# Masked attention with an int8 linear layer: maxima from float32 q and k in row groups, jobs in column groups, fixed PSUM banks

## The chip, the core and the metric

The kernel runs on one core of a Trainium2 chip. Five engines work side by side, each through its own queue in order: TensorE (PE in the profile; its weight loads are PEld), VectorE (DVE), ScalarE (ACT), GpSimd (POOL) and SyncE (SP), which issues most DMAs. PSUM, where TensorE writes its results, has eight banks of 128 partitions x 512 float32. The metric is the device time of one execution in microseconds (us), less being better; it is given as the median of several runs.

## The reference

Eight batches of x (512 channels x 1024 tokens) go through attention with 16 heads of 32 channels under a key mask; the result is quantised per row to int8, multiplied by an int8 weight, scaled, and added to x.

```python
Q, K, V = (proj(Wq), proj(Wk), proj(Wv))           # (B, 16, 1024, 32) each
att = einsum('bhqd,bhkd->bhqk', Q, K) / sqrt(32) + b
att = att * m + (1.0 - m) * -1e30
y = einsum('bhqk,bhkd->bhqd', softmax(att), V)     # back to (B, 512, 1024)
q, in_scale = per_token_quant_int8(y)              # absmax / 127 of each row
out = einsum('bsk,nk->bsn', q, weight) * in_scale * w_scale + bias
return x + out.astype(float16)
```

## The kernel before

**Tiling.** Four heads (128 channels) of one batch are a group: 8 x 4 = 32 groups. A group has two halves X of 512 queries, and a half has eight steps, one for each chunk of 128 keys: 512 steps s in all, 16 to a group. The main loop (L907) goes by pairs of steps.

**A step.** `scores` (L433) writes four heads' scores, keys on partitions, into two tiles of two banks. For each head a bfloat16 matmul with ones (L450) first puts in the query's maximum (`shift`, split into three bfloat16 parts), then a float32 matmul adds k times q (L455). The heads lie in four groups of 32 rows of the array, so four matmuls run abreast. ACT takes the exponential of 128x1024 at a time (L464) into e. `add_up` (L476) adds the e of a half on POOL, 128x2048 at a time, in seven of its eight steps. `product` (L489) multiplies by V, each head in its own group of 32 columns, accumulating over the eight steps of a half in one bank. `half_denominators` (L505) sums the columns of the half's sum; DVE copies (L515), takes reciprocals (L543) and multiplies y (L546).

**Maxima ahead of the scores.** The query's maximum over the keys must be known before its scores are. `maxima` (L371) computes the scores once more with queries on partitions, in units of one head and 128 queries: two matmuls over all 128 rows in float32r. For that q and k are split into a high and a low part (`evict`, L236: ACT writes the high part and the full one, DVE the low part), and DMAs stack them into 128 rows per head (`stack_head`, L339, ks and qs). `take_maxima` (L402) is one DVE operation per unit, which adds the mask and reduces 1024 keys, with the result read out of an accumulator by a second, small instruction. A step has two units. `split_tops` (L422, L424) cuts a half's maxima into three bfloat16 parts on POOL, and `place_tops` transposes them by a DMA on SP (L429).

**Jobs.** The projections of later groups (`project`, L211, `project_v`, L311) and the linear layer of the group before last (`linear`, L716) are cut into pieces and laid between the maxima, as matmuls over the full array. One piece of a pair runs in column groups instead (`columns`, L199), behind the product. Float32 matmuls appear as two instructions each. ACT or DVE move the results out of PSUM. Later steps quantise y on ACT (L595 to L601), and POOL adds bias and x (L699, L700).

**Order.** All five engines run in the order in which the program is written (`manual_schedule`). PSUM is four pools: two tiles of two banks for scores and some maxima (ps_s), one of two banks for other maxima and the denominators (ps_m), one bank for the product (ps_av), one for jobs (ps_job).

Of the kernel before, what the change touches and what calls it, by code (L numbers as in the profile page):

```python
# [20 lines left out]
P = 128  # L21
# [3 lines left out]
QUARTER = 256  # L25
# [8 lines left out]
def kernel(  # L34
# [15 lines left out]

# [11 lines left out]
    UH = HG * HN  # L83
    last = n_groups - 1
    ON_ARRAY = n_steps - NT - HN
    BY_TURNS = n_steps - NT - 2
# [3 lines left out]
    xpool = ctx.enter_context(tc.tile_pool(name="x", bufs=5))  # L90
    mpool = ctx.enter_context(tc.tile_pool(name="mask", bufs=2))
    qkpool = ctx.enter_context(tc.tile_pool(name="qk", bufs=2))
    stack = ctx.enter_context(tc.tile_pool(name="stack", bufs=4))
    epool = ctx.enter_context(tc.tile_pool(name="e", bufs=3))
    small = ctx.enter_context(tc.tile_pool(name="small", bufs=2))
    work = ctx.enter_context(tc.tile_pool(name="work", bufs=1))
    ps_s = ctx.enter_context(tc.tile_pool(name="ps_s", bufs=2, space=PSUM))
    ps_m = ctx.enter_context(tc.tile_pool(name="ps_m", bufs=1, space=PSUM))
    ps_av = ctx.enter_context(tc.tile_pool(name="ps_av", bufs=1, space=PSUM))
    ps_job = ctx.enter_context(tc.tile_pool(name="ps_job", bufs=1, space=PSUM))  # L100

    def bank(name, dtype=F32, shape=(P, HALF)):
        return ps_job.tile(list(shape), dtype, tag="job", name=name)


# [8 lines left out]
    def load_w(i, which):  # L114
        cols = slice(i % NG * P, (i % NG + 1) * P)
        name, src = (("wq", wqT), ("wk", wkT))[which]
        w = const.tile([P, NG, P], F32, tag=name, name=f"{name}_{i}")
        nc.sync.dma_start(w, src[:, cols].rearrange("(c p) o -> p c o", p=P))
        w_qk[i, which] = w
# [32 lines left out]
    bias_sb = const.tile([P, N], F32, tag="bias", name="bias_sb")  # L152

# [8 lines left out]

# [8 lines left out]

# [17 lines left out]


    full = {}
    splits = {}

    def columns(acc, weights, moving, **kwargs):

        for r in range(0, P, DH):
            nc.tensor.matmul(acc[r : r + DH], weights[:, r : r + DH], moving, **kwargs)  # L199

    def project(i, which, h, quarters=(0, 1), by_chunk=False):


        b, g = divmod(i, NG)
        w = w_qk[i, which]

        def piece(a, c, matmul=nc.tensor.matmul):
            acc = jobs["bank"]
            cols = slice(a * QUARTER, (a + 1) * QUARTER)
            place = slice((a - quarters[0]) * QUARTER, (a - quarters[0] + 1) * QUARTER)  # L210
            matmul(  # L211
                acc[:, place],
                w[:, c, :],
                x_sb[b, c][:, h * HALF : (h + 1) * HALF][:, cols],
                start=(c == 0 and (a == 0 or not by_chunk)),
                stop=(c == NG - 1 and (a == quarters[-1] or not by_chunk)),
            )
            if (a, c) == (quarters[-1], NG - 1):
                cols = slice(quarters[0] * QUARTER, (a + 1) * QUARTER)
                evict(i, which, h, cols, acc[:, : place.stop])  # L220

        order = [(a, c) for a in quarters for c in range(NG)]
        if by_chunk:
            order.sort(key=lambda o: o[1])
        return [lambda *x, a=a, c=c: piece(a, c, *x) for a, c in order]

    def split_tiles(i, which, h):
        name = "qk"[which]
        high = work.tile([P, HALF], F32R, tag=f"{name}h{h}", name=f"{name}h_{i}_{h}")
        low = work.tile([P, HALF], F32R, tag=f"{name}l{h}", name=f"{name}l_{i}_{h}")  # L230
        splits[i, which, h] = high, low
        full[i, which, h] = qkpool.tile(
            [P, HALF], F32, tag=f"{name}{h}", name=f"{name}f_{i}_{h}"
        )

    def evict(i, which, h, cols, acc):  # L236
        if (i, which, h) not in splits:
            split_tiles(i, which, h)
        high, low = (t[:, cols] for t in splits[i, which, h])
        top = masks[i // NG][1]  # L240
        for dst in (high, full[i, which, h][:, cols]):
            if which == 0:
                nc.scalar.activation(dst, acc, AF.Copy, scale=top)  # L243
            else:
                nc.scalar.copy(dst, acc)

        early = jobs["early"]

        def rest():
            if early:  # L250

                f = full[i, which, h][:, cols]
                nc.gpsimd.tensor_tensor(low, f, high.bitcast(F32), ALU.subtract)
            elif which == 0:
                nc.vector.scalar_tensor_tensor(
                    low, acc, top, high.bitcast(F32), ALU.mult, ALU.subtract
                )
            else:
                nc.vector.tensor_tensor(low, acc, high.bitcast(F32), ALU.subtract)

        later.append(rest)

    def first_projections():

        k0, k1 = (ps_s.tile([P, HALF], F32, tag="s", name=f"kps_0_{h}") for h in range(NH))
        accs = [(0, 0, bank("qps_0")), (1, 0, k0), (1, 1, k1)]

        order = [(c, a) for c in (0, 1) for a in accs[1:]] + [(c, accs[0]) for c in (0, 1)]
        order += [(2, a) for a in accs[1:] + accs[:1]] + [(NG - 1, a) for a in accs]

        warm = ps_av.tile([P, P], F32, tag="av", name="warm")
        for _ in range(WARM):
            nc.tensor.matmul(warm, ones_b, ones_b, start=True, stop=True)
# [8 lines left out]
        top = masks[0][1]  # L282
        for which, h, acc in accs:
            split_tiles(0, which, h)
            f = full[0, which, h]
            if which == 0:
                nc.scalar.activation(f, acc, AF.Copy, scale=top)
            else:
                nc.vector.tensor_copy(f, acc)
        prepare_mask(0, 2)  # L290
        for which, h, _ in accs[1:] + accs[:1]:
            high, low = splits[0, which, h]
            nc.scalar.copy(high, full[0, which, h])
            nc.gpsimd.tensor_tensor(low, full[0, which, h], high.bitcast(F32), ALU.subtract)
# [3 lines left out]
    def project_v(i, quarters, offset=0):  # L298

        b, g = divmod(i, NG)  # L300
        KQ = QUARTER // P

        def piece(a, r, matmul=nc.tensor.matmul):
            if i not in v_sb:
                v_sb[i] = work.tile([P, NT, P], F32, tag="v", name=f"v_{i}", bufs=2)
            acc = jobs["bank"]
            t, part = divmod(r, 2)
            k = a * KQ + t
            place = offset + (k - quarters[0] * KQ) * P
            for c in range(part * NG // 2, (part + 1) * NG // 2):  # L310
                matmul(  # L311
# [6 lines left out]
            if (a, r) == (quarters[-1], 2 * KQ - 1):  # L318
                keys = slice(quarters[0] * KQ, (a + 1) * KQ)
                copies.append(  # L320
                    lambda: nc.scalar.copy(  # L321
                        v_sb[i][:, keys, :].rearrange("p k c -> p (k c)"),
                        acc[:, offset : place + P],
                    )
                )

                if offset == 0:
                    flush(copies)

        return [lambda *x, a=a, r=r: piece(a, r, *x) for a in quarters for r in range(2 * KQ)]  # L330

    stacks = {}

    def stack_tile(i, j, which):
        stacks[i, j, which] = stack.tile(
            [P, T], F32R, tag="qk"[which], name=f"{'qk'[which]}s_{i}_{j}"
        )

    def stack_head(i, j, which, h, engine=nc.sync):  # L339
        order = ((0, 0, 1, 1), (0, 1, 0, 1))[which]  # L340
        if (i, j, which) not in stacks:
            stack_tile(i, j, which)
        s = stacks[i, j, which]
        for a, part in enumerate(order):
            engine.dma_start(  # L345
                s[a * DH : (a + 1) * DH, h * HALF : (h + 1) * HALF].bitcast(F32),
                splits[i, which, h][part][j * DH : (j + 1) * DH, :].bitcast(F32),
            )

# [3 lines left out]
    def maxima_bank(k):  # L353


        first = k < -FIRST * HN
        turn = k < HALF_FIRST and k % 3 != 1
        pool, tag = (ps_s, "s") if (turn if first else k % HN in (1, 2)) else (ps_m, "m")
        return pool.tile([P, NH, HALF], F32, tag=tag, name=f"mps_{k}")

    def maxima(k):
        X, u = divmod(k, UH)
        i, h = divmod(X, NH)
        j, n = divmod(u, HN)
        q, kk = stacks[i, j, 0], stacks[i, j, 1]
        if u == 0:
            tops[X] = small.tile([P, HN, HG], F32, tag="tops", name=f"tops_{X}")
        acc = maxima_bank(k)
        n0 = h * HN + n
        for a in range(NH):  # L370
            nc.tensor.matmul(  # L371
                acc[:, a, :],
                q[:, n0 * P : (n0 + 1) * P],
                kk[:, a * HALF : (a + 1) * HALF],
                start=True,
                stop=True,
            )
        take_maxima(k, acc, X, j, n)
# [667 lines left out]
```

## Time and profile before

| what | value |
|---|---|
| median of 3 runs | 2527.62 us (2527.54 to 2527.64) |
| profiled execution, first to last instruction | 2525.2 us |
| TensorE, clock granted over the span | 0.999 of full speed |
| scores of the first step start | 46.05 us |
| last exponential starts | 2503.3 us |
| first sum of a half (POOL), 63 records | from 53.5 to 2450.7 us |
| one exponential (ACT, 128x1024) | 1111 ns, 1024 of them |
| one sum (POOL, 128x2048) | 4566 ns |
| one maximum (DVE, 128x1024) | 1224 ns, 1024 of them |
| one reciprocal (DVE, 128x128) | 924 ns, 252 of them |

"Busy" is the time in which an engine has an instruction under way; the matmuls' ends are modelled, so a run of matmuls is best measured from one start to the next. A group of instructions is shown as line, engine, operation, what is written and read with shapes, count, busy time in us and mean ns of one, and behind the last bar the idle time of the engine before them, with what ended it.

### The profile page before, as it was taken

To read this page: it belongs to the slowest core of one execution; us is meant where nothing else is said; L and a number is where in the kernel's file an instruction comes from. 1 tells how busy PE (TensorE), PEld (TensorE's weight loads), DVE (VectorE), ACT (ScalarE), POOL (GpSimd) and SP (SyncE) were. 2 spreads that over 40 slices of the span, in tenths; PEclk is the share of its full clock that TensorE was granted. 3 is DMA by queue.
4 is the path that set the end of the run, shared out by engine and by line. 5 is a ranking of instruction groups with operands and counts; after the bars stand their busy time and mean duration, and the time that the engine had idled before them with its cause. 6 is when DMAs were issued, how large, how long until landed. Compare 5 with 4: busy or idle time off the path is not lost.

```text
span 2525.2 us, 50860 instructions
## 1 busy us (share of the span) xinstructions
PE 2500.8 (99%) x19444; PEld 1431.3 (57%) x19444; DVE 1805.5 (71%) x2901; ACT 1474.3 (58%) x1653; POOL 2245.5 (89%) x906
## 2 busy tenths in 40 slices
PE   9999999999999999999999999999999999999998
PEld 5555555555556565555555555655555555555542
DVE  5567777777777777777777777777776777777775
ACT  3556666556665556665556665566655566556654
POOL 2988999999999999999999999999999999999992
PEclk9999999999999999999999999999999999999999
DMA  5333333343333433334333343333433334333331
GB/s 160 81 80 96 96 88 83 88 113 85 90 77 92 113 79 86 89 91 113 80 83 92 85 117 82 77 87 96 116 81 79 83 102 107 86 78 81 83 76 45
DMA packets 225953, 228.10 MB, mean 90 GB/s; under 512 B 104368, under 2 KB 138160, under 8 KB 225712
## 3 DMA queue, kind: packets, MB, share of 16 engines
q1 hardware_dynamic: 225136, 224.06, 34.6%
q8 instruction: 156, 2.56, 0.4%
q10 hardware_dynamic: 576, 0.79, 0.1%
q14 instruction: 85, 0.70, 0.1%
HBM read 57.70 MB, written 16.78 MB: 29 GB/s over the span
## 4 chain that ended last, share of the span: by engine, by line
POOL 67%; PE 20%; issue 11%; SPq 1%; DMA 1%; ACT 1%; DVE 0%; POOLq 0%; DVEq 0%
POOL sum L476 58%; PE mps L371 4%; PE av L489 4%; PE sps L455 3%; PE job L211 3%; POOL o L700 3%; POOL o L699 3%; PE job L311 2%; PE sps L450 2%; POOL part L422 1%; POOL tops L424 1%; PE job L716 1%; SPq L345 1%; PE job L199 0%; PE dps L505 0%
## 5 line engine op out<-in xcount | busy, mean ns | idle before, releaser
L476 POOL TENSOR_TENSOR sum<-sum,e 128x2048 f32<-128x2048 f32 x374 | 1707.9, 4566 | 28.6 <-ACT e L464 9.5
L402 DVE CUSTOM_DVE_ANT_0 rest<-mps,row 128x1024 bf16<-128x1024 f32 x1024 | 1253.3, 1224 | 597.8 <-PE mps L371 363.0
L464 ACT ACTIVATE e<-sps,kbias 128x1024 f32<-128x1024 f32 x1024 | 1085.7, 1111 | 451.4 <-PE sps L455 425.0
L371 PE MATMUL mps<-ks,qs 128*128 128x512 f32 x2032 | 763.7, 457 | 8.6 <-ACT e L464 7.0
L455 PE MATMUL sps<-qf,kf 32*128 32x512 f32 x4096 | 549.5, 589 | 0.0
L489 PE MATMUL av<-e,v 128*32 128x512 f32 x4096 | 494.3, 598 | 0.0
L371 PEld LDWEIGHTS mps<-ks,qs 128*128 128x128 f32 x2032 | 332.7, 190 | 235.5 <-DVE den L515 94.5
L476 POOL TENSOR_TENSOR sum<-e,e 128x2048 f32<-128x2048 f32 x63 | 286.4, 4546 | 140.7 <-ACT e L464 137.9
L489 PEld LDWEIGHTS av<-e,v 128*32 128x32 f32 x4096 | 107.4, 109 | 346.0 <-issue 345.0
L311 PEld LDWEIGHTS job<-wv,x 128*128 128x128 f32 x1884 | 258.1, 191 | 27.3
L311 PE MATMUL job<-wv,x 128*128 128x128 f32 x1884 | 260.1, 274 | 0.0
L211 PE MATMUL job<-x,wq 128*128 128x256 f32 x914 | 246.4, 378 | 0.0
L450 PE MATMUL sps<-shift,ones_b 32*128 32x512 bf16 x2048 | 229.0, 383 | 3.2 <-DVE tops L402 1.4
L543 DVE RECIPROCAL den<-den 128x128 f32<-128x128 f32 x252 | 224.9, 924 | 0.0
L211 PE MATMUL job<-x,wk 128*128 128x256 f32 x854 | 223.8, 378 | 0.0
L455 PEld LDWEIGHTS sps<-qf,kf 32*128 32x128 f32 x4096 | 207.4, 183 | 4.5
L211 PEld LDWEIGHTS job<-x,wq 128*128 128x128 f32 x914 | 172.3, 189 | 34.3
L321 ACT COPY v<-job 128x256 f32<-128x256 f32 (+1 forms) x95 | 41.8, 442 | 253.4 <-PE job L311 253.4
L211 PEld LDWEIGHTS job<-x,wk 128*128 128x128 f32 x854 | 161.2, 189 | 30.8
L450 PEld LDWEIGHTS <-ones_b 32*128 32x128 bf16 x2048 | 69.4, 91 | 182.1 <-issue 164.4
L243 ACT ACTIVATE qh<-job,top 128x256 fp32r<-128x256 f32 (+1 forms) x91 | 49.8, 547 | 174.5 <-PE job L211 149.1
L716 PE MATMUL job<-w_sb,qT 128*128 128x256 bf16 (+1 forms) x944 | 126.4, 276 | 0.0
(110 smaller groups left out, 1439.8 us busy)
## 6 DMA issues: line engine op xcount, KB each, us to landing
ks<-kh SPq DMA_DIRECT2D x508, 64.0 KB, 2.0
ks<-kl SPq DMA_DIRECT2D x508, 64.0 KB, 2.0
qs<-qh SPq DMA_DIRECT2D x506, 64.0 KB, 2.0
qs<-ql SPq DMA_DIRECT2D x506, 64.0 KB, 2.0
x<-in_x SPq DMA_DIRECT2D x32, 512.0 KB, 4.9
xr<-in_x SPq DMA_DIRECT2D x62, 256.0 KB, 3.4
out<-o SPq DMA_DIRECT2D x62, 256.0 KB, 3.3
wk<-in_wkT SPq DMA_DIRECT2D x32, 256.0 KB, 3.7
```

The lines of the kernel that those rows point to most:

```text
L211: matmul(acc[:, place], w[:, c, :], x_sb[b, c][:, h * HALF : (h + 1) * HALF][:, cols], start=(c == 0 and (a == 0 or not by_chunk)), stop=( ...
L311: matmul(acc[:, place : place + P], x_sb[b, c][:, k * P : (k + 1) * P], wv_sb[:, c, g * P : (g + 1) * P], start=(c == 0), stop=(c == NG - 1),)
L371: nc.tensor.matmul(acc[:, a, :], q[:, n0 * P : (n0 + 1) * P], kk[:, a * HALF : (a + 1) * HALF], start=True, stop=True,)
L402: nc.vector.tensor_tensor_reduce(out=rest, in0=acc.rearrange("p h t -> p (h t)"), in1=row, scale=-1.0, scalar=HIGH, op0=ALU.add, op1=ALU.m ...
L450: nc.tensor.matmul(accs[j // 2][:, j % 2, :], ones_b[r, :], shift[r, :], start=True, stop=False)
L455: nc.tensor.matmul(accs[j // 2][:, j % 2, :], k[r, k0 * P : (k0 + 1) * P], q[r, :], start=False, stop=True,)
L464: nc.scalar.activation(e[:, 2 * a : 2 * a + 2, :], acc, AF.Exp, bias=kbias[:, kc : kc + 1], scale=SCALE)
L476: nc.gpsimd.tensor_tensor(sums[X], other, exps[s], ALU.add)
L489: nc.tensor.matmul(accs_av[X][r, :], v_sb[i][:, kc, r], exps[s][:, j, :], start=(kc == 0), stop=(kc == NT - 1),)
L543: nc.vector.reciprocal(d[:, cols], source[:, cols])
L699: engine.tensor_tensor(o16[:, c], o[:, c], bias_sb[:, half][:, c], ALU.add)
L716: matmul(acc, qT[:, k, :], w8_sb[:, k, half][:, cols], start=(k == 0), stop=(k == NT - 1),)
```

## The change

**PSUM.** One pool holds four tiles of a single bank (one[0] to one[3]) and two tiles of a pair of banks (two[0], two[1]) for the whole run. An even step's scores go to one[0], one[1] and two[1], an odd step's to one[2], one[3] and two[1]; the maxima of that step go to the other two singles and to two[0]. When the exponentials have read a step's singles, the product of an even step takes the first, and the step's job the other one.

**Maxima.** Each step has one unit of two heads and 128 queries: four float32 matmuls of 32 rows straight from q and k, behind the scores. For the second half of the keys they read copies in which the heads are turned by 64 rows (`turn_heads`, three copies per group, two DMAs each), so that the four matmuls use four row groups. The splits, the stacks and their DMAs are gone. Maxima run LEAD = 11 steps ahead of the scores. Where a head's two halves lie in single banks, DVE takes them in two operations, one into tops[X][0] and one into tops[X][1]; the latter is first filled by a memset on POOL. `split_tops` moves from POOL to DVE and starts with the smaller of the two.

**Jobs and product.** The product of two steps is made in every even step, into a fresh bank; ACT copies the first of a half into y, and DVE adds the other three. All jobs run in column groups, behind the product in even steps (linear, denominators) and behind the maxima in odd ones (three pieces of 128 columns of projections). ACT copies the denominators. The exponential is three operations: two of one bank, one of a pair. e has five buffers in place of three, x eight in place of five, weights two in place of one. From eleven steps before the end on, no maxima are left, and products and denominators are made step by step.

```diff
-    ps_s = ctx.enter_context(tc.tile_pool(name="ps_s", bufs=2, space=PSUM))
...
+    psum = ctx.enter_context(tc.tile_pool(name="psum", bufs=1, space=PSUM))
+    one = [psum.tile([P, HALF], F32, tag=f"one{a}", name=f"one{a}") for a in range(4)]
+    two = [psum.tile([P, NH, HALF], F32, tag=f"two{a}", name=f"two{a}") for a in range(2)]
+    def score_banks(s):
+        a = 0 if s >= TAIL else s % 2
+        return one[2 * a : 2 * a + 2], two[1 - s % 2 if s >= TAIL else 1]
+    def maxima_banks(s):
...
+        return [one[2:] if s % 2 == 0 else one[:2], halves(two[0])]
...
+        for a in range(2):
+            nc.sync.dma_start(t[a * 2 * DH : (a + 1) * 2 * DH, :], f[(1 - a) * 2 * DH : (2 - a) * 2 * DH, :])
...
+    def project(i, which, h, cols, acc):
+        b, g = divmod(i, NG)
+        for c in range(NG):
+            columns(
+                acc,
+                w_qk[i, which][:, c, :],
+                x_sb[b, c][:, h * HALF : (h + 1) * HALF][:, cols],
+                start=(c == 0),
+                stop=(c == NG - 1),
+            )
...
+    def maxima(m, accs):
+        X, u = divmod(m, NT)
+        i, h = divmod(X, NH)
+        pair, n = divmod(u, HN)
+        for a in range(NH):
+            turn = a if m >= EARLY else 0
+            q = turned[i, 0][h] if turn else full[i, 0, h]
+            k = turned[i, 1] if turn else full[i, 1, a]
+            for j in range(2):
+                r = ((pair + turn) % 2 * 2 + j) * DH
+                nc.tensor.matmul(
+                    accs[j][a],
+                    q[r : r + DH, n * P : (n + 1) * P],
+                    k[r : r + DH, :],
...
+    def take_maxima(m, accs):
...
+        if u == 0:
+            tops[X] = [
+                small.tile([P, HN, HG], F32, tag=f"tops{a}", name=f"tops{a}_{X}") for a in range(NH)
+            ]
+            nc.gpsimd.memset(tops[X][1], HIGH)
+        for j in range(2):
+            apart = accs[j][0].tensor is not accs[j][1].tensor
+            for a in range(NH if apart else 1):
...
+                nc.vector.tensor_tensor_reduce(
+                    out=rest[:, keys],
+                    in0=accs[j][a] if apart else both(accs[j]),
+                    in1=row[:, keys],
...
+                    accum_out=tops[X][a][:, n, 2 * pair + j : 2 * pair + j + 1],
...
-        engine = nc.vector if X == 0 else nc.gpsimd
+        engine = nc.vector
+        engine.tensor_tensor(left, left, other, ALU.min)
...
+    def keep_product(X, first, acc):
...
+        if first:
+            nc.scalar.copy(y, acc)
+        else:
+            nc.vector.tensor_tensor(y, y, acc, ALU.add)
...
+        X, u = divmod(s + 3, NT)
+        if u == 0 and 0 <= X < n_halves:
+            split_tops(X)
+            place_tops(X)
...
+        if s >= 0:
+            scores(s)
+            exponentials(s)
             add_up(s)
+        m = s + LEAD
+        if m < n_steps:
+            maxima(m, maxima_banks(s))
+            take_maxima(m, maxima_banks(s))
...
+        elif s > 0 and s % 2 == 0:
+            acc = score_banks(s)[0][0]
+            for a in (2, 1):
+                product(s - a, acc, a == 2, a == 1)
+            keep_product((s - 2) // NT, (s - 2) % NT == 0, acc)
+        if s >= 0:
+            multiply()
+        for (_, keep, args, cols, _), place in zip(items, places):
+            keep(*args, cols, place)
+        load_ahead(i, t)
+        if i >= 0:
+            rest_of(i, t)
```

In a group, with t the step in it: projections run in odd steps; denominators in steps 2 and 12; linear pieces of 256 columns in steps 4, 6, 8 and 10; reciprocals in steps 5, 6, 6, 7 and 13, 14, 14, 15; y is multiplied in steps 8 and 0; the largest of y and its scale follow in step 8; ACT quantises in steps 10, 12, 14 and 0; POOL adds bias and x at the start of steps 7 and 11; the split of the maxima stands at the start of steps 5 and 13, and a new half's first unit of maxima in the same steps.

## The prediction

> **What bounds the kernel now.** I read the page's parts 1 and 4 first, then the costliest groups, then the timelines of TensorE and VectorE in the middle of the run, then the DMA queue's waits.
>
> ```profile
> PE 2500.8 (99%) x19444; PEld 1431.3 (57%) x19444; DVE 1805.5 (71%) x2901; ACT 1474.3 (58%) x1653; POOL 2245.5 (89%) x906
> ...
> POOL 67%; PE 20%; issue 11%; SPq 1%; DMA 1%; ACT 1%; DVE 0%; POOLq 0%; DVEq 0%
> ...
> L476 POOL TENSOR_TENSOR sum<-sum,e 128x2048 f32<-128x2048 f32 x374 | 1707.9, 4566 | 28.6 <-ACT e L464 9.5
> L402 DVE CUSTOM_DVE_ANT_0 rest<-mps,row 128x1024 bf16<-128x1024 f32 x1024 | 1253.3, 1224 | 597.8 <-PE mps L371 363.0
> ```
>
> The chain names POOL for 67%, yet POOL idles about 2 us in each half where no sum is due, while PE is busy 99%. The list of PE's waits holds 7.0 us as its longest entry. So PE is the bound, with POOL close behind. DVE sat idle 363.0 us waiting for PE's maxima: it has slack now. PE's prices, from its timeline (start, length, line; a next start ends a piece):
>
> ```profile
> 1227.54 1.92 PE L489 MATMUL av<-e,v 128*32 128x512 f32 x16
> 1229.28 0.61 PE L505 MATMUL dps<-sum,ones_f 128*32 128x256 f32 x8
> 1229.83 0.39 PE L450 MATMUL sps<-shift,ones_b 32*128 32x512 bf16 x4
> 1230.05 1.03 PE L455 MATMUL sps<-qf,kf 32*128 32x512 f32 x8
> 1231.01 0.73 PE L371 MATMUL mps<-ks,qs 128*128 128x512 f32 x2
> ...
> 1238.73 0.62 PE L199 MATMUL job<-wv,x 128*32 128x128 f32 x16
> 1239.29 0.40 PE L450 MATMUL sps<-shift,ones_b 32*128 32x512 bf16 x4
> ```
>
> Two steps of the V product take 1.74 us (1227.54 to 1229.28): four 512-column float32 matmuls abreast cost **0.87**. Scores take **1.18** with the turn to the next mode (1229.83 to 1231.01). L505 and L199 take 0.55 and 0.56 before the scores; half of 0.87 is 0.43, so the turn from column to row groups costs **0.12**. L199 is the piece of a job that already runs in column groups: 16 matmuls of 128 columns cost what 8 of 256 do. The first sum of a half repeats 63 times from 53.5 to 2450.7 us: 38.66 us per half, **77.3 per group** of 16 steps.
>
> **PE after.** Per group: scores 16 x 1.18 = 18.9; maxima as four float32 matmuls in four row groups, the form of L455, 16 x 0.87 = 13.9 (no turn, they follow the scores); product 13.9; projections, six halves (q, k, v) x 4 chunks x 0.87 = 20.9; linear 32 x 0.107 = 3.4 (a 256-column pass; L199's 0.43 is four of them); denominators 2 x 0.87 = 1.7; turns 16 x 0.12 = 1.9. Sum **74.7**, that is 4.78 in a step with a job, 3.91 in steps 0 and 14. Against 77.3 PE gains 2.6 us. Unknown: a long run of 128-column pieces in column groups (64 passes for V), of which the trace has four in a row. Bounds: 0.107 as in L199, or 0.137 as in L311's 128-column matmuls, which wait for weights (260.1 us over 1884 records): 0 to +1.9 a group, or 60 us in all. I take 0, L199 being the same form.
>
> **Removed at no gain.** The 2028 SP issues that fill ks and qs, the second eviction on ACT, the low parts on DVE (L255, L259) and the denominators' copies (L515, now on ACT) leave queues that did not set the end; their cover was PE's work. ACT's 128x1024 exponential becomes 0.59 + 0.59 in place of 1.11 for one of two (0.59: the 128x512 copy of L245): +36 us in all on an engine busy 58%, beside PE. The six turning DMAs of a group are few; the tightest, k's second half, is kept after step 3's jobs and read in step 5's maxima, about 5.9 us later, of which 0.7 goes to the eviction, 1.1 to two issues and 2.0 to landing (the ks rows): 2.1 spare. Later weights, x, residual and mask loads, and the transposes, pass the SP queue at a step's slack or more; ACT's quantising sits behind the exponentials. Cost 0, in the cover of a 4.8 us step.
>
> **DVE after.** A 1024-column maximum starts 1.38 us after the one before, and another kind of operation 1.15 after it:
>
> ```profile
> 1223.69 1.22 DVE L402 CUSTOM_DVE_ANT_0 rest<-mps,row 128x1024 bf16<-128x1024 f32 x1
> ...
> 1225.07 1.23 DVE L402 CUSTOM_DVE_ANT_0 rest<-mps,row 128x1024 bf16<-128x1024 f32 x1
> ...
> 1226.45 1.22 DVE L402 CUSTOM_DVE_ANT_0 rest<-mps,row 128x1024 bf16<-128x1024 f32 x1
> 1227.60 0.08 DVE L402 DVE_READ_ACCUMULATOR2_ANT tops<- 128x1 f32 x1
> 1227.60 0.48 DVE L728 SCALAR_TENSOR_TENSOR o<-job,scale,ws_sb 128x256 f32<-128x256 f32 x1
> ```
>
> One of the two pairs now lies in single banks and takes two 512-column operations. No row has that; the reductions of L555 differ by 0.52 between 1024 and 512 columns, so 0.70, plus the 0.15 between two: 0.85 (from 0.61, half the old cost, to 1.38, no saving). A step takes 0.85 + 0.85 + 1.15 = **2.85**. Further: y added in three of four even steps, 0.65 (L259, 0.69, less the overlap); split_tops now here, 6 x about 0.22 = 1.35 in steps 5 and 13; reciprocals 0.9; multiplying y 0.95 (0.80 to 1.1); largest and scale 1.55; a linear piece 0.45. Steps 5 to 8 need 5.1 + 5.75 + 3.75 + 6.45 = 21.05 against PE's 19.1; steps 13, 14, 15, 0 need 5.1 + 5.3 + 3.75 + 4.45 = 18.6 against 17.4. PE can't run ahead: each step's maxima write pair two[0], which the last step's third DVE operation reads. So **3.1** late. Where y's addition and a linear piece follow each other, the single banks come free 0.87 + 0.3 + 2.85 + 0.65 + 0.45 + 0.06 = 5.18 after the maxima began, 0.4 over a step: 0.5 more a group in steps 4 and 10, up to 1.6 where steps 6 and 8 have no other lateness.
>
> **The new wait.** take_maxima fills tops[X][1] by a memset on POOL at the first unit of each half, in steps 5 and 13, after add_up of that step has been put on POOL's queue. The second DVE operation writes into that tile, so it must follow. POOL works in order; small work behind its sums waits long now:
>
> ```profile
> SPq L429 <- POOL part L422: 517.0, 63, 15.0
> ```
>
> The transpose of the maxima waits 517.0 / 63 = 8.2 us for POOL's 0.26 us casts. There it has slack; here DVE, and behind DVE's queue PE, wait. From step 5's scores at 0: exponentials start at 1.35 (1207.06 to 1208.41 in the timeline) and last 2.29, so 3.64; the sum 4.57 + 0.07: 8.3; memset 0.1 (L142): 8.4; second operation 0.85, third 1.22, the signal 0.06: PE's next maxima start at 10.55 in place of 4.78 + 1.18 = 5.96, **4.6** late. At step 13 POOL is behind: add_residual in step 11 takes 1.29 + 1.49, so sums 11 to 13 end 6.45 + 3 x 4.64 = 20.4 after step 11, 10.8 after step 13: **7.1** late. Within these waits the splits cost nothing, so DVE's lateness falls from 3.1 to 0.6, with 1.6 of bank waits. Bounds of the wait: 0 if nothing holds the write, 11.7 in full; I take it in full, since both engines write the same bytes. Next late are scores, exponentials and sums of step 6; POOL's own work (14 x 4.64 + 2 x 2.8 = 70.6) then idles too, so nothing is caught up.
>
> Group: 74.7 + 0.6 + 1.6 + 11.7 = **88.6**, 11.3 over 77.3.
>
> **The clock.** PE stands still some 3.5 us in the first wait and 6 in the second. At the end of the run the granted clock (the column after POOL) falls 2.4 us after the last matmul (2516.6):
>
> ```profile
> 2518.00:2519.00 1.00, 0.00 (x0) 0.00 (x0) 0.96 (x2) 0.00 (x0) 0.92 (x2) 1.00 0.37 139
> 2519.00:2520.00 1.00, 0.00 (x0) 0.00 (x0) 1.00 (x1) 0.00 (x0) 0.70 (x1) 0.52 0.00 0
> 2520.00:2521.00 1.00, 0.00 (x0) 0.00 (x0) 0.93 (x3) 0.00 (x0) 0.67 (x1) 0.50 0.44 174
> ```
>
> By that row both waits may halve the clock. How long it stays low no row shows; the 40 matmuls of the start last 4.18 us at 104 ns, twice what 128 columns take at 0.107 per 256, so at most some 4.2 us at half speed, 2.1 lost. Bounds: 0 to 62 x 2.1 = 130; much lies under DVE's work after the wait, so I take **50**. The Trainium skill, "TensorE: Matmul & The Clock Gate", Part 1, says that the gate looks at free-running windows of about 3.4 us, and throttles after one that is idle. By that rule the shorter wait seldom trips it and the longer mostly does: an estimate of half, some 25 to 65 us; the row would have both trip.
>
> **The ends.** Before, the first scores start at 46.05; now eleven steps of maxima (15 x 1.38 + 7 x 1.70 = 32.6 on DVE, the last of them beside the scores) make it about +3. The last group loses its projections and keeps its 3.04 us tail steps: -5. Sum: 2525.2 + 31 x 11.3 - 2 = 2873; with 2.4 outside the span (median 2527.6) 2876; with the clock **2925**. Its own range: 2780 (the waits half filled with other work) to 3070 (full clock loss and V at 0.137).
>
> **Rivals.** *The memset holds nothing up* (it runs early, or DVE isn't made to wait): 74.7 + 3.1 + 0.5 = 78.3, 2525.2 + 31 - 2 + 2.4 = **2557**. For: POOL has 2 us of idle time per half; against: that lies at the half's start, not at step 5. *PE stays the bound and gets its gain*: DVE's lateness fits into the slack of the banks and the memset holds nothing: 74.7, so 2525.2 - 31 x 2.6 - 2 + 2.4 = **2445**, faster. It decides if all waits of a group stay under 2.6 us. For: DVE's 363 us of waiting for PE; against: steps 5 to 8 overdraw DVE by 2 us alone. *The maxima don't run four abreast*: 0.87 becomes 1.74, +13.9 per group, **3350**; against: each pair's second half reads turned heads, so four row groups are named.
>
> **Chances.** Forecast 0.86, memset harmless 0.07, PE's gain 0.05, not abreast 0.02. Within 0.2% (what a measurement here can tell) lies only a part of the second: faster 0.05, same 0.02, slower 0.93. 2780 to 3070 holds nine tenths of the forecast; stretched down to 2700 for waits that are partly covered, 0.8 of all.
>
> **What would show it.** Right: a group's period near 89 us; DVE idle before the maxima with POOL's memset as releaser, about 62 times 5 us or more; PE's longest waits on DVE's maxima; sums of clock below 1.00 after them. Wrong: no such releaser, PE busy near 99%, or a V piece in column groups far from 0.107 per pass. The prediction falls if the memset runs ahead of the sum.

## The result, and the profile after

| kernel | median us | runs | span of the profiled one | clock granted |
|---|---|---|---|---|
| before | 2527.58 (2527.18 to 2527.64) | 4 | 2525.2 | 0.999 |
| after | 3054.84 (3051.82 to 3056.09) | 4 | 3052.0 | 0.933 |

The ratio is 1.2086, with a 95% interval of 1.2069 to 1.2103: slower by a fifth. The page of the changed kernel, busy time (share of the span) by engine, the chain that ended last, and some of its costliest groups:

```profile
PE 2642.6 (87%) x35007; PEld 1218.2 (40%) x35008; DVE 2358.7 (77%) x4208; ACT 1523.0 (50%) x2166; POOL 2146.4 (70%) x650
...
PE 65%; DVE 29%; issue 5%; DVEq 0%; ACT 0%; POOL 0%; DMA 0%; SPq 0%; POOLq 0%
...
L375 POOL TENSOR_TENSOR sum<-sum,e 128x2048 f32<-128x2048 f32 x374 | 1698.9, 4543 | 513.3 <-ACT e L365 506.9
...
L303 DVE CUSTOM_DVE_ANT_0 rest<-one,row 128x512 bf16<-128x512 f32 x1018 | 698.8, 686 | 546.8 <-PE one L281 308.3
...
L346 PE MATMUL one<-shift,ones_b 32*128 32x512 bf16 x1024 | 245.8, 406 | 360.5 <-DVE tops L303 357.7
...
L325 DVE TENSOR_TENSOR tops<-tops,part 128x16 f32<-128x16 f32 x128 | 290.9, 2273 | 4.4
```

TensorE is down from 99% to 87% and waits 357.7 us before the first matmul of scores (L346), for VectorE's maxima (L303). POOL, which the chain named for 67% before, is at 0%, and VectorE has 29%. The last line is the odd one: a subtraction of 128x16 elements takes 2273 ns in the mean, where a maximum over 128x512 takes 686. VectorE's groups show its companion, `split_tops`' minimum (L320), and the conversion between them (L323):

```profile
L320 DVE TENSOR_TENSOR tops<-tops,tops 128x16 f32<-128x16 f32 x64 | 205.6, 3212 | 0.0
...
L323 DVE CAST part<-tops 128x16 bf16<-128x16 f32 x192 | 47.5, 247 | 6.6
```

Where in a group it happens is seen from the starts of the scores' L346 matmuls into the pair of banks, the last that they fill: the difference from one step to the next, mean over 28 groups in the middle of the run, in us.

```
step     0    1    2    3    4     5    6    7    8    9   10   11   12    13   14   15    sum
after 3.94 5.57 4.80 4.84 4.81 10.48 6.83 4.94 4.81 5.07 5.08 4.82 4.80 12.07 5.64 5.36  93.86
```

Steps 5 and 13, where `split_tops` runs and the memset is issued, have 5.67 and 7.26 us over 4.81; steps 6 and 14 behind them have 2.02 over 4.81 and 1.73 over the 3.91 forecast for a step without a job. These are put down to the waits and to the clock. (The L346 matmul into the first bank starts 0.87 us earlier behind a wait; by it steps 5 and 6 would have 9.61 and 7.70. The line between the two shares is a choice, their sum isn't.) The remainder of the group is 93.86 - 12.93 - 3.75 = 77.2.

The timeline of VectorE, POOL and TensorE in one step 5 (start, length, line):

```profile
1487.33 4.54 POOL L375 TENSOR_TENSOR sum<-sum,e 128x2048 f32<-128x2048 f32 x1 [0.30 <-ACT e L365]
...
1489.56 2.35 DVE L320 TENSOR_TENSOR tops<-tops,tops 128x16 f32<-128x16 f32 x1
...
1490.75 2.83 PE L186 MATMUL one<-wv,x 128*32 128x128 f32 x96
...
1492.14 4.52 POOL L375 TENSOR_TENSOR sum<-sum,e 128x2048 f32<-128x2048 f32 x1 [0.27 <-ACT e L365]
1492.18 4.52 DVE L325 TENSOR_TENSOR tops<-tops,part 128x16 f32<-128x16 f32 x1
...
1496.60 0.11 POOL L297 MEMSET tops<- 128x16 f32 x1
1496.73 0.20 DVE L323 CAST part<-tops 128x16 bf16<-128x16 f32 x1
...
1497.27 0.68 DVE L303 CUSTOM_DVE_ANT_0 rest<-one,row 128x512 bf16<-128x512 f32 x1
```

The minimum starts at 1489.56 and ends at 1491.91, as POOL's sum does (1491.87); the first subtraction starts at 1492.18, just behind the next sum, and ends at 1496.70, the sum at 1496.66. Only then do VectorE's maxima begin. Of the split's 192 operations with two inputs in SBUF (L320, L325) 123 began while a sum of POOL's ran, and each of these ended 29 to 47 ns after that sum; the other 69 took 0.18 us in the median. Of y's additions (L395), which read one input from PSUM, 122 began beside a sum and took 0.68 to 0.69 us all the same. The memset ran at 1496.60, when VectorE was still held; no wait of VectorE's for L297 is in the trace. The windows of the same place (from:to, length, busy time of PE, PEld, DVE, ACT, POOL, the clock granted, the DMAs' share and GB/s) show the clock in the column after POOL:

```profile
1497.00:1498.00 1.00, 0.00 (x0) 0.00 (x0) 0.93 (x4) 0.00 (x0) 0.00 (x0) 1.00 0.00 0
1498.00:1499.00 1.00, 0.48 (x5) 0.20 (x7) 0.72 (x3) 0.00 (x0) 0.00 (x0) 0.78 0.33 68
1499.00:1500.00 1.00, 1.00 (x8) 0.72 (x9) 1.00 (x1) 0.00 (x0) 0.00 (x0) 0.50 0.50 94
...
1501.00:1502.00 1.00, 1.00 (x11) 0.34 (x4) 0.08 (x1) 0.94 (x2) 0.00 (x0) 0.52 0.07 14
1502.00:1503.00 1.00, 1.00 (x15) 0.27 (x12) 0.58 (x1) 1.00 (x2) 0.00 (x0) 1.00 0.01 4
```

TensorE's last matmuls end near 1493.6 and it resumes at 1498.0. In this group its clock halves 0.5 us after that, for 3.41 us by the trace's clock record. In the next group TensorE stands still from 1586.8 to 1591.2; there the clock halves 0.5 us before it resumes and stays low for 6.83 us:

```profile
1590.00:1591.00 1.00, 0.00 (x0) 0.00 (x0) 0.93 (x4) 0.00 (x0) 0.00 (x0) 0.86 0.00 0
1591.00:1592.00 1.00, 0.58 (x1) 0.10 (x1) 0.83 (x4) 0.00 (x0) 0.00 (x0) 0.50 0.09 19
...
1597.00:1598.00 1.00, 1.00 (x12) 0.24 (x8) 0.86 (x3) 0.00 (x0) 1.00 (x1) 0.73 0.00 0
```

The two patterns take turns from group to group.

### The profile page after: what moved, and what is told of

It reads as the page before. It is cut to its first block, busy times and chain, and to the rows that moved or that the text cites. A ratio compares the mean times of both kernels' runs of the same rounds, so it can differ in the third digit from the quotient of the medians.

```text
span 3052.0 us, 80925 instructions
## 1 busy us (share of the span) xinstructions
PE 2642.6 (87%) x35007; PEld 1218.2 (40%) x35008; DVE 2358.7 (77%) x4208; ACT 1523.0 (50%) x2166; POOL 2146.4 (70%) x650
## 4 chain that ended last, share of the span: by engine, by line
PE 65%; DVE 29%; issue 5%; DVEq 0%; ACT 0%; POOL 0%; DMA 0%; SPq 0%; POOLq 0%
PE one L186 21%; PE one L281 13%; PE one L351 12%; PE one L383 10%; DVE tops L325 10%; DVE rest L303 8%; DVE tops L320 7%; PE one L346 5%; PE two L281 2%; DVE part L323 2%; DVE y L395 1%; PE one L401 1%; DVE tops L303 1%; DVE o L526 0%; PE two L351 0%
## 5 line engine op out<-in xcount | busy, mean ns | idle before, releaser
L365 ACT ACTIVATE e<-one,kbias 128x512 f32<-128x512 f32 x1024 | 647.7, 684 | 989.5 <-PE two L351 497.8
L303 DVE CUSTOM_DVE_ANT_0 rest<-one,row 128x512 bf16<-128x512 f32 x1018 | 698.8, 686 | 546.8 <-PE one L281 308.3
L303 DVE CUSTOM_DVE_ANT_0 rest<-two,row 128x1024 bf16<-128x1024 f32 x515 | 630.5, 1224 | 77.3 <-PE one L281 2.1
L351 PE MATMUL one<-qf,kf 32*128 32x512 f32 x2048 | 603.1, 651 | 0.0
L281 PE MATMUL one<-kf,qf 32*128 32x512 f32 x1022 | 573.6, 643 | 28.6 <-DVE y L395 27.2
L281 PE MATMUL two<-kt,qt 32*128 32x512 f32 x1026 | 582.4, 652 | 0.0
L351 PE MATMUL two<-qf,kf 32*128 32x512 f32 x2048 | 579.2, 646 | 0.0
L281 PE MATMUL one<-kt,qt 32*128 32x512 f32 x1014 | 577.9, 651 | 0.0
L281 PE MATMUL two<-kf,qf 32*128 32x512 f32 x1034 | 577.7, 643 | 0.2 <-DVE tops L303 0.2
L365 ACT ACTIVATE e<-two,kbias 128x1024 f32<-128x1024 f32 x512 | 571.3, 1116 | 0.0
L346 PE MATMUL one<-shift,ones_b 32*128 32x512 bf16 x1024 | 245.8, 406 | 360.5 <-DVE tops L303 357.7
L346 PEld LDWEIGHTS <-ones_b 32*128 32x128 bf16 x2048 | 64.3, 91 | 631.5 <-issue 631.5
L325 DVE TENSOR_TENSOR tops<-tops,part 128x16 f32<-128x16 f32 x128 | 290.9, 2273 | 4.4
```

Source lines behind the costliest of these rows:

```text
L281: nc.tensor.matmul(accs[j][a], q[r : r + DH, n * P : (n + 1) * P], k[r : r + DH, :], start=True, stop=True,)
L303: nc.vector.tensor_tensor_reduce(out=rest[:, keys], in0=accs[j][a] if apart else both(accs[j]), in1=row[:, keys], scale=-1.0, scalar=HIGH, ...
L325: engine.tensor_tensor(left, left, piece, ALU.subtract)
L346: nc.tensor.matmul(accs[j], ones_b[r, :], shift[r, :], start=True, stop=False)
L351: nc.tensor.matmul(accs[j], k[r, k0 * P : (k0 + 1) * P], q[r, :], start=False, stop=True,)
L365: nc.scalar.activation(part, acc, AF.Exp, bias=kbias[:, kc : kc + 1], scale=SCALE)
```

## The experiments

The theories: **memset** (VectorE's write into tops[X][1] follows POOL's memset, which stands behind a sum: the forecast, theory M below) and **split** (operations of VectorE with two SBUF inputs are held until POOL's sum ends: theory P). A time without an interval is that of one run.

**e1: the memset by VectorE.**

```diff
-            nc.gpsimd.memset(tops[X][1], HIGH)
+            nc.vector.memset(tops[X][1], HIGH)
```

> The changed kernel with one edit: the memset of tops[X][1] is made by DVE instead of POOL. Theory M (the prediction's: the memset behind POOL's sums is what holds DVE): the 11.7 us per group go, 2557 to 2600 us. Theory P (DVE's operations with two inputs in SBUF, the minimum and the subtractions of split_tops, are held while a POOL sum runs; the memset ends in the same moment and hides): same as the changed kernel, 3035 to 3060 us, the subtractions still up to 4.5 us long.

Measured: 3053.16 us, the group 93.95. The memset alone, as sole cause, falls.

**e2, e3, e4: both suspects taken out, then each put back.** Out they go where no head's two halves lie in separate tiles: the four singles become halves of two pair tiles, one 1024-column operation takes each head, and neither memset nor minimum is left.

```diff
-    one = [psum.tile([P, HALF], F32, tag=f"one{a}", name=f"one{a}") for a in range(4)]
+    duo = [psum.tile([P, NH, HALF], F32, tag=f"one{a}", name=f"one{a}") for a in range(2)]
+    one = [duo[a // 2][:, a % 2, :] for a in range(4)]
...
-        engine = nc.vector
-        engine.tensor_tensor(left, left, other, ALU.min)
+        engine = nc.vector if X == 0 else nc.gpsimd
```

e3 sets `engine = nc.vector` again; e4 keeps e2's split and adds a memset of the one tops tile on POOL.

> The four single banks become halves of two pairs, so DVE takes each head's 1024 keys in one operation (1.38 + 1.15 = 2.53 us a step in place of 2.85), the second tops tile, its memset and the minimum go, and split_tops is back on POOL. Neither wait is left. Both theories: PE is the bound, 74.7 to 76 us per group, 2445 to 2490 us, faster than both kernels; granted clock back to 1.00. If DVE's load alone (and not a wait on POOL) were the cause, it would stay above 2600.

> As e2, with split_tops left on DVE: no memset, but two subtractions with both inputs in SBUF per half. Theory M: as e2, 2445 to 2500 us. Theory P: the subtractions wait for a running sum, one to two of them per half (2.4 to 8.8 us per half against 0.2 each): 2750 to 3000 us, mean of the subtraction's line 2 us or more.

> As e2 (split_tops on POOL), with a memset of the half's maxima on POOL put back in front of the first maximum. This measures the predicted wait alone. Theory M: 4.6 + 7.1 us per group and the clock's loss: 2800 to 2900 us, DVE's maxima waiting some 60 times for the memset's line. If the memset doesn't hold DVE: as e2, 2445 to 2490 us.

Measured: e2 2956.35 (ratio 1.1691, 1.1667 to 1.1714), e3 2974.48, e4 3305.68 us. e2 missed its expectation by far, though its long steps are gone (clock 0.997). Nearly every step is longer instead, about 6.5 in even ones and 5.4 in odd ones, 91.46 a group; TensorE's waits show why (us in total, times, longest):

```profile
PE one L187 <- ACT e L362: 141.2, 248, 1.0
PE one L380 <- ACT e L362: 135.4, 249, 0.8
PE one L187 <- DVE y L392: 82.5, 87, 1.3
```

As one tile, the two banks come free together: the product waits for both exponentials, a job for y's addition in the other half. So the base is disturbed, and e3 against e2 (+18) says little: on that slower schedule only 2 of the 128 subtractions began beside a sum. e4 does speak: +349, and VectorE waited 546.2 us in 62 times for the memset. The memset's wait is real where nothing else hides it.

**e5, e6, e7: the same question on the banks of the changed kernel.** The second operation of a head starts from the first one's result, so one tops tile is enough.

```diff
+                top = tops[X][0][:, n, 2 * pair + j : 2 * pair + j + 1]
...
-                    scalar=HIGH,
+                    scalar=top if a else HIGH,
...
-                    accum_out=tops[X][a][:, n, 2 * pair + j : 2 * pair + j + 1],
+                    accum_out=top,
...
-        engine = nc.vector
-        engine.tensor_tensor(left, left, other, ALU.min)
+        engine = nc.vector if X == 0 else nc.gpsimd
```

e6 is e5 with `nc.gpsimd.memset(tops[X][0], HIGH)`; e7 is e5 with `engine = nc.vector`.

> Single banks as in the changed kernel. The second operation of a head starts from the first one's result, so there is one tops tile, no memset and no minimum, and split_tops is on POOL again. Nothing of DVE then waits for POOL. Both theories, from the changed kernel's step lengths with steps 5, 6, 13 and 14 at the length of their neighbours: 78 to 80 us per group, 2540 to 2610 us, the prediction's rival of 2557; granted clock above 0.99. If a third wait in the change mattered, it would stay above 2650.

> As e5, with a memset of the half's maxima put on POOL in front of the first maximum, behind the step's sum: the predicted wait alone, no split on DVE. Theory M prices it at 11.7 us per group over e5 plus the clock, 2900 to 2990 us. If the memset is free: as e5.

> As e5, with split_tops on DVE: two subtractions per half with both inputs in SBUF, no minimum, no memset. Theory P (held until the running sum ends): 2 to 7 us per half in steps 5 and 13, 2700 to 2950 us, subtractions of up to 4.5 us. If only the memset matters: 2540 to 2610 us.

```
step     0    1    2    3    4     5    6    7    8    9   10   11   12    13   14   15    sum
e5    3.94 5.63 4.80 4.84 4.81  5.20 4.81 5.20 4.81 5.14 5.15 4.82 4.80  5.14 3.90 5.68  78.64
e6    3.94 5.63 4.80 4.84 4.81 11.12 7.09 4.84 4.81 5.14 5.15 4.82 4.80 12.79 5.45 5.56  95.58
e7    3.94 5.63 4.80 4.84 4.81 10.32 6.84 4.99 4.81 5.15 5.13 4.82 4.80 12.05 5.75 5.37  94.03
```

Measured: e5 2576.09 (ratio 1.0188, 1.0174 to 1.0202, clock 0.997), e6 3108.27, e7 3058.94 us. With neither suspect the loss of 527 us is down to 48. With **either alone** it is back in full, in the same steps; both times lie above the ranges expected. e6's memset isn't quite the changed kernel's, where only the second operation of a half writes the tile that is filled: in e6 the first does too. So e6 shows that such a wait is real and what it costs there, not a share of the 527 us. In e6 VectorE's waits name the memset; in e7 its groups show the split's conversions (L320) and subtractions (L322) held, about 0.2 us each where nothing holds them:

```profile
DVE rest L302 <- POOL tops L295: 574.3, 62, 11.2
```
```profile
L320 DVE CAST part<-tops 128x16 bf16<-128x16 f32 x192 | 345.0, 1797 | 4.5
L322 DVE TENSOR_TENSOR tops<-tops,part 128x16 f32<-128x16 f32 x128 | 188.7, 1474 | 4.4
```

**e8: the minimum alone stays on VectorE** (memset on VectorE, the rest of the split on POOL).

```diff
-        engine = nc.vector
-        engine.tensor_tensor(left, left, other, ALU.min)
+        engine = nc.vector if X == 0 else nc.gpsimd
+        nc.vector.tensor_tensor(left, left, other, ALU.min)
```

> The changed kernel with the memset on DVE and the casts and subtractions of split_tops on POOL; only the minimum of the two tops tiles stays on DVE, one operation with both inputs in SBUF per half. Theory P: held once per half, 2.4 us in step 5 and 4.5 in step 13 as in the changed kernel, so 5 to 7 us per group over e5: 2700 to 2800 us. If DVE's small operations aren't held: as e5, 2540 to 2620 us.

Measured: 2612.28 us, less than expected. The minimum was held as long as before (mean 3206 ns), but steps 5 and 13 came to 5.13 and 6.78: one hold fits nearly into VectorE's slack. What ruins the changed kernel is the chain: the minimum waits for one sum, the subtraction behind it starts 40 ns into the next sum (in the step 5 shown above) and waits for that one too.

**e9, e10, e11: what is left of e5, and a version under both kernels.** e9 only moves VectorE's work; e10 moves the jobs (below) and, against e5, lays reciprocals and the products of y earlier (steps 3, 3, 4, 5 and 6 in place of 5, 6, 6, 7 and 8); e11 is e10 with one product of y moved.

> The same kernel as e5 (second operation starts from the first one's result, splits on POOL), with VectorE's other work laid only behind odd steps: reciprocals of a half two at a time in steps 3, 5 and 13, 15, the products of y and the reciprocals in steps 7 and 1, the row's largest value in step 9. In e5 these lie in even steps too, behind y's addition, and TensorE waits 40.2 us in 67 times for y and its steps 5, 7, 9, 10, 13 and 15 take 5.14 to 5.68 us in place of 4.80. Theory (what is left in e5 over TensorE's own 4.8 per step is VectorE's lateness where its work is heaped): group 75.5 to 76.5 in place of 78.64, so 2480 to 2515 us, under the kernel before. Rival (the banks' order sets the rest, wherever VectorE's work lies): 2560 to 2580, as e5. TensorE's waits for y fall under 15 us by the first and stay near 40 by the second.

Measured: 2574.09 us (1.0181, 1.0168 to 1.0195), the group 78.59; waits for y 41.2 us. The theory falls, its rival holds: the banks set the rest. y's addition follows three maxima in even steps, and the next maxima need all three of the banks then read.

```diff
-        for a in range(NT):
-            steps[2 * a + 1] = row[3 * a : 3 * a + 3]
+        for t, a, b in ((0, 0, 1), (1, 1, 4), (3, 4, 7), (4, 7, 8), (5, 8, 10), (6, 10, 11), (7, 11, 13), (8, 13, 14), (9, 14, 16), (11, 16, 18), (13, 18, 21), (14, 21, 22), (15, 22, 24)):
+            steps[t] = row[a:b]
...
-                    steps[4 + 4 * h + 2 * a] = [piece]
+                    t = ((5, 7), (9, 10))[h][a]
+                    steps[t] = steps.get(t, []) + [piece]
```

The row of projection pieces is the same, and `add_residual` follows its linear pieces by a step.

> e5 with its jobs laid out anew. In e9 TensorE still waits 0.35 us in steps 5, 7, 9, 13 and 0.85 in 1 and 15: a step's maxima need the banks that VectorE's work of the even step before reads last (three maxima, y's addition, a linear piece: 5.0 us after the maxima of that step began), and steps 0 and 14 give it only 3.9 us. Here one projection piece each goes from the odd steps to steps 0, 4, 6, 8 and 14, and the linear pieces go to 5, 7, 9 and 10, where y isn't added; the two short steps are 11 and 15. Theory (the banks, held by VectorE's chain in even steps, set what is left): steps 4.80 but for two of 3.9 to 4.0, group 75.0 to 76.0 in place of 78.6, 2465 to 2505 us, faster than the kernel before. Rival (the array itself is slower than my sum where jobs are mixed, or POOL with some 72 us per group now holds): 2530 to 2580.

> e10 with one more move. e10's steps came to 4.8 to 5.0 us as its theory said, but for steps 7 and 8, 6.40 and 5.87: there VectorE's product of y and the reciprocals, an operation with two inputs in SBUF as the split's, began beside POOL's running sum and took 3.9 to 4.0 us in place of 0.68. Here this product of the second half moves from step 6 to step 8, whose VectorE work ends where POOL has no sum (from step 9 + 0.4 to step 9 + 3.7 in e10), and the row's largest value to step 9. Theory (the product was held by POOL's sum): it takes 0.7 us there, steps 7 and 8 fall to 4.8 to 4.9, group 76.0 to 76.8 in place of 79.1, 2490 to 2515 us, faster than the kernel before. Rival (steps 7 and 8 are long for the jobs that are mixed there, three kinds in one bank): they stay over 5.8 us, 2560 to 2590.

```
step     0    1    2    3    4     5    6    7    8    9   10   11   12    13   14   15    sum
e10   5.05 4.82 4.82 4.84 4.81  4.93 4.86 6.40 5.87 4.88 4.96 3.95 5.02  5.14 4.77 3.96  79.09
e11   5.05 4.81 4.82 4.84 4.81  4.94 4.86 4.88 5.02 4.90 4.96 3.97 5.01  5.14 4.77 3.97  76.73
```

Measured: e10 2584.73 (1.0221, 1.0207 to 1.0236), e11 2516.81 us (0.9955, 0.9941 to 0.9968). e10's steps came down as its theory said, but for 7 and 8, and its timeline shows the hold once more, in an operation that the change did not touch:

```profile
1504.54 9.49 POOL L372 TENSOR_TENSOR sum<-sum,e 128x2048 f32<-128x2048 f32 x2
...
1505.18 0.68 DVE L392 TENSOR_TENSOR y<-y,one 128x512 f32<-128x512 f32 x1
1505.78 3.86 DVE L435 TENSOR_TENSOR y<-y,den 128x512 f32<-128x512 f32 x1
```

Two operations of one shape, one behind the other, beside the same sum: y's addition reads one operand from PSUM and takes its usual 0.68; y times the reciprocals reads both from SBUF and takes 3.86. Moved to where POOL has no sum, it takes 0.96 at this place of the run and 1.25 to 1.30 in most groups, ending 0.55 us after POOL's addition of x (L518), beside which it now begins; and steps 7 and 8 fall by 2.4 us together, as the theory said (the last group of lines is VectorE's, of e5, e10 and e11 in turn: mean of both halves' products; the first half's is still held in e11, 2.3 us in a step that has the slack):

```profile
L435 DVE TENSOR_TENSOR y<-y,den 128x512 f32<-128x512 f32 x64 | 46.8, 732 | 0.2
```
```profile
L435 DVE TENSOR_TENSOR y<-y,den 128x512 f32<-128x512 f32 x64 | 191.9, 2998 | 0.2
```
```profile
L435 DVE TENSOR_TENSOR y<-y,den 128x512 f32<-128x512 f32 x64 | 111.7, 1746 | 0.2
```

e11 beats the kernel before by 0.45% (0.32 to 0.59), though it lies just above the range expected: a part of the change's gain in TensorE's work was there to be had.

## Why the prediction was right in its end and wrong in a step

3054.84 lies in the range (2700 to 3070), near its upper end, and the direction was right. By group, in us:

| term | forecast | measured |
|---|---|---|
| TensorE's work, VectorE's lateness, banks | 74.7 + 0.6 + 1.6 = 76.9 | 77.2 |
| wait in steps 5 and 13 | 4.6 + 7.1 = 11.7 | 5.67 + 7.26 = 12.9 |
| lost to the clock | 50 / 31 = 1.6 | 2.02 + 1.73 = 3.75 |
| sum | 90.2 | 93.86 |

31 groups of 3.66 make 113 of the 130 us between forecast and result. The other 17 lie mostly in the ends, which I took as -2: span less 31 groups is 128.6 before and 142.3 after, so +14.

**The step that failed** is "split_tops now here, 6 x about 0.22 = 1.35", and its consequence, "Within these waits the splits cost nothing". In the groups of before the one VectorE operation with two SBUF inputs is y times the reciprocals (L546), and none of its 64 began beside a sum, so no row showed the price. Measured, with the mean of each kind, a split is 3.21 + 2 x 2.27 + 3 x 0.25 = 8.5 us, and that, not the memset, is what the trace shows ahead of the maxima. The sign I named, VectorE idle with POOL's memset as releaser 62 times, is missing for that reason: VectorE counts as busy while it is held. The trace of before had the hint all the same: L546 (128x512) took 1.45 us at 1489.41 and 0.79 at 1450.87, and ended both times 0.54 to 0.55 us after POOL's addition of the bias, beside which it had begun, the first time soon after that operation's start and the second near its end. I used 0.80 to 1.1 as its price and did not ask what the difference was.

```profile
1489.01 1.30 POOL L699 TENSOR_TENSOR o<-o,bias_sb 128x512 f16<-128x512 f32 x1
1489.41 1.45 DVE L546 TENSOR_TENSOR y<-y,den 128x512 f32<-128x512 f32 x1
```

The size came out nevertheless, for a reason that e6 and e7 show: the memset's wait is real (e6 costs 532 us over e5, e7 483), and both waits end with the same sum of POOL's. I had not foreseen that: as far as the split goes, the right size was luck. Whichever an engine is made to wait for, the end of that sum sets the maxima. They lie side by side and don't add up, so e1 alone would have cleared the memset wrongly.

The Trainium skill, "SBUF — State Buffer", "Who interferes with whom", has the rule that I should have weighed: VectorE and GpSimd share a pair of ports as an exclusive lock, a VectorE operation with two SBUF inputs contends with a GpSimd operation that reads SBUF, and whichever issues first keeps the pair for its whole length. The trace agrees in its 123 holds that end with the sum, and in y's addition, which reads PSUM and keeps its 0.68 us beside it. The same section lists copies and casts among the operations that can enter a mode that takes both ports; e7's conversions, 1797 ns in the mean, agree. As an estimate by that rule, the price of the first operation alone is up to a whole sum, 4.54 us, and of a chain of them up to one sum each.

**The clock.** The forecast took 50 us out of 0 to 130; measured are some 3.75 x 31 = 116, if all of the excess in steps 6 and 14 is the clock's. The clock record bears that out: from the scores' restart at the pair of banks to the end of the low stretch it is 3.1 and 5.4 us by turns after step 5, 4.3 and 2.9 after step 13; half of that is 1.5, 2.7, 2.2 and 1.4, and the excess measured is 1.5, 2.6, 2.1 and 1.4. Two terms were mis-sized. "At most some 4.2 us at half speed" fails, since 45 of the 67 low stretches last 6.83 us, 18 last 3.41 and three 10.24. And "much lies under DVE's work" fails: of 23.9 us of low clock in two groups 8.1 lie before the scores' restart, and the rest shows in the steps at its full price. Of the two answers weighed, the row's was right: a low stretch follows each of the 62 waits, the shorter ones too. The rule of free-running windows of about 3.4 us, "TensorE: Matmul & The Clock Gate", Part 1, fits these lengths and the turns: step 6 takes 7.4 us where the low stretch is 6.83 and 6.3 where it is 3.41. As an estimate, two groups are 187.7 us, 55.0 windows of 3.413, and in e6, whose group of 95.58 us is 28.0 of them, step 6 takes about 7.1 us in every group; that the windows hold the groups to these lengths no run here shows.

**Right:** TensorE's step of 4.78 (4.80 to 4.84 in undisturbed ones) and the step without a job, 3.91 (3.94, 3.90); V in column groups at 0.107 per pass (96 matmuls in the 2.56 us that their weight loads last); the half maximum, 0.70 (0.686); the 5.18 us after which the banks come free (5.14 to 5.20 in e5's steps 5, 7, 9, 13). The half exponential was 0.63 to 0.68 in place of 0.59, on an idle engine. **Right in size for another reason:** VectorE's "3.1 late" in steps 5 to 8 and 13 to 0. Without the two waits a group has 3.9 us over 74.7, but e9 lays that work apart and gains nothing, while e11, which moves the jobs as well, gains half of it (76.73): it was the banks after y's addition, above all 0.85 in steps 1 and 15, behind the two short steps, which I had not seen. **The rivals:** "the memset holds nothing up", 2557, is what e5 measures with both waits gone, 2576: some 10 us of the difference lie in the groups (78.64 for 78.3), the rest in the ends; its condition, that a memset behind the sum holds nothing, falls with e4 and e6. "PE gets its gain", 2445, was never near: e5's waits for banks take 3.9 of a group against a gain of 2.6; e11 has it in part, with 76.73 against 77.31 before. "The maxima don't run four abreast", 3350, falls with the undisturbed steps of 4.80.

## What to carry to other kernels

Before moving small operations to VectorE, look at which of their operands lie in SBUF and what POOL runs beside them: the price is POOL's remaining time, not their own, and the page counts it as busy. A wait that costs much may hide a second that ends with the same event, so take out both and put each back alone. When a bound is lifted, look for work that can be moved between steps before the queue's order is taken as given.

## What was not expected of the hardware

A held operation ends with the sum, whatever its size: those of 128x16 elements 29 to 47 ns after it, with up to 4.52 us in place of 0.18, and y's products of 128x512 0.55 us after it (e10, e11). In the waits of 4.4 us without matmuls the clock fell either 0.5 us before TensorE resumed, for 6.83 us, or 0.5 us after, for 3.41 us, so that nearly all of the loss falls on work. Two banks in one tile are waited for as one: e2, which differs from e5 in this and in taking each head's maxima in one operation, took 380 us more.
